# Row-group packing in the folds and the small attention, the score's two readers in the other order, and chunk 6's last sums ahead of the last finish

## The chip, the cores and the metric

The kernel runs on one core of one Trainium2 chip (trn2). The metric is device time in microseconds (us) of one launch; lower is better. The kernel before the change has a median of 2024.21 us over three runs (2023.55 to 2026.4).

TensorE (PE in the profile) multiplies matrices into PSUM, VectorE (DVE) and ScalarE (ACT) read PSUM and compute, GpSimd (POOL) computes on SBUF, and SyncE (SP) issues transfers. Each engine works through its own queue in order.

## The reference

Everything is float32. `x` is 16 samples of 64 latents of width 128 (1024 tokens), `ctx_1024` is 16 samples of 1601 context rows of width 128. Two layers run after each other:

```python
x = x + xattn0(ctx_1024, layernorm(x))            # 16 heads of 64; keys = context and latents
x = x + scan0(layernorm(x))                       # selective scan, width 256, 16 states
x = x + moe(layernorm(x))                         # small attention (4 heads of 32, one shared K and V), then top-2 of 8 experts
x = x + xattn1(ctx_1024, layernorm(x), mask)      # as xattn0, with a mask on context rows
x = x + scan1(layernorm(x))                       # convolution, 4 heads of 64, state 64
x = x + ffn(layernorm(x))                         # weights and activations quantized to fp4 in blocks of 16
```

For the change two pieces matter. The cross attention's projections are folded first: per head, `Wq_h Wk_h^T` and `Wv_h Wo_h` are 128x128 matrices, each a product over 64 rows. The small attention in `moe` is

```python
Q = (nx @ Wq.T) in 4 heads of 32;  K = nx @ Wkc.T;  V = nx @ Wvc.T     # K, V: 32 wide, the same for all heads
out = softmax(Q K^T / sqrt(32)) V per head;  X = X + concat(out) @ Wo.T
```

over samples of 64 tokens.

## The kernel before

The kernel is one program without loops on the chip; Python writes out every instruction. The tokens are 8 chunks of 128 (two samples each). The cross attention has 64 groups: 2 layers x 16 samples x 2 halves of the heads. A group has 13 context tiles of 128 rows (`NT`), and 8 heads x 64 latents make 512 columns (`NQ`).

`run` counts ticks `n`. Each tick (`step`) writes one tile's score (`scores`, L638 on: a matmul of 512 columns into one of three PSUM buffers of the pool `pss`) and, 21 ticks later (`LAG`), four matmuls of 129 columns that average the context with the weights of a tile (`average`). In between, a group's running maximum is turned (`maximum`, L674), spread (`mb`, L692), subtracted (L700) and exponentiated (L701).

A score in PSUM has two readers. ScalarE copies it to SBUF as `st` (L656 with the mask of layer 1, L658 in layer 0), and VectorE takes it into the running maximum `R` (L663 with the mask, L665 without). Both read the same PSUM bank, and the tile framework puts two readers from different engines on one bank in the order in which they are written: the copy first, then the maximum. The buffer is free for the score three ticks later when both are through.

Other work is written by generators between ticks. `prep` holds what the attention needs (latents, queries, context tiles, folds), `between` holds the stages after it: `scan0` and `moe` for four groups of two chunks in layer 0, then `scan1` and `ffn` in layer 1 for chunks 0-1, 2-3, 4-5, 6 and 7. A generator's `yield` gives a due time in ticks or a cost against a budget. Instructions written under `behind` may not be placed ahead of the last tick's. These stages use PSUM tiles of the pool `pst` (`tp`, three buffers that go round).

`fold` (L329 on) makes the folded matrices, four heads at a time: 2 layers x 2 products x 4 groups of heads. `raw_pair` loads 64 rows of four heads to 64 partitions; four matmuls over 64 rows (L341) fill one PSUM tile, and one instruction of 512 columns brings it out (L344 on ScalarE for the first two, else L346 on VectorE).

The small attention of `moe` works on two chunks (256 tokens, 4 samples). Queries are made per head on 32 partitions (`mq`, L929: 4 matmuls of 256 columns); keys (`mk`, L936) and values (`mv`, L940) follow. Scores `ms` (L951) are 8 matmuls over 32 rows, weights are turned (`mt`, L970), averaged (`ma`, L979: 8 matmuls over 64 rows with 32 output rows), copied (L982) and projected (`mo`, L988: 8 matmuls over 32 rows, four added up for each chunk).

At the end, `finish` (L726 on) brings the last group's average out, turns it and adds the output projection `o` (L785) to X. After the last tick `run` takes the remaining stages in turn: `tails` holds the chain of chunk 7's `scan1` and `ffn`, and the chain of what is left of chunk 6. Chunk 6's `ffn` ends with four matmuls `fo` (L1399), a sum into X (L1400) and the store (L1401). Chunk 7's `scan1` begins with a layer norm: `bn_stats` (L144), POOL's power (L135) and the scaling (L162). `fill` (L130) are matmuls without a use[...].

Of the kernel before, what the change touches and what calls it, by code (L numbers as in the profile page):

```python
# [32 lines left out]
F32 = mybir.dt.float32  # L33
# [3 lines left out]
AF = mybir.ActivationFunctionType  # L37
# [5 lines left out]
P = 128  # L43
# [30 lines left out]
CG = 2  # L74
# [5 lines left out]
class Kernel:  # L80
# [79 lines left out]
    def scaled(self, eng, dst, src, mv, r, n):  # L160
        for c in range(n):
            eng.tensor_scalar(dst[:, c, :], src[:, c, :], mv[:, c, 0:1], r[:, c:c + 1], ALU.subtract, ALU.mult)  # L162
# [154 lines left out]
    def raw_pair(self, lay, l, r, g, queue):  # L317


        if lay == 0:  # L320
            t = self.at.tile([P, 2, NQ], F32, tag="st2", name=f"raw{l}{g}", bufs=11)
            pair = [t[:DH, i, :].rearrange("p (h d) -> p h d", h=4) for i in range(2)]
        else:
            pair = [self.at.tile([DH, 4, D], F32, tag="raw", name=f"raw{n}{g}", bufs=3) for n in (l, r)]
        for t, n in zip(pair, (l, r)):
            queue.dma_start(out=t, in_=self.a[f"L{lay}{n}"].rearrange("(h j) d -> j h d", j=DH)[:, g * 4:g * 4 + 4, :])
        return pair

    def fold(self, lay, dst, l, r, scale):  # L329

        nc = self.nc
        for g in range(H // 4):
            if (lay, l) == (0, "WqT"):
                raw = self.raw0[g]
            else:
                raw = self.raw_pair(lay, l, r, g, nc.sync)
            if lay == 0 and l == "WvT":
                yield HOP3
            t = self.tp(f"{l}{lay}{g}")
            for k in range(4):  # L340
                nc.tensor.matmul(t[:, k * D:(k + 1) * D], raw[0][:, k, :], raw[1][:, k, :], start=True, stop=True)  # L341
# [296 lines left out]
    def scores(self, g, i):  # L638
# [15 lines left out]
        if masked:  # L654
            mc = self.mcol[:, i, b:b + 1]
            ev = nc.scalar.activation(st, s, AF.Identity, bias=mc)  # L656
        else:
            ev = nc.scalar.copy(st, s)  # L658
        self.place["ACT"].append(ev.ins)
        if i:  # L660
            last = grp["st"][0][:, 0, :] if i == 1 else R
            if masked:
                mx = nc.vector.scalar_tensor_tensor(R, s, mc, last, ALU.add, ALU.max)  # L663
            else:
                mx = nc.vector.tensor_tensor(R, s, last, ALU.max)  # L665
            self.place["DVE"].append(mx.ins)

# [236 lines left out]
    def moe(self, gr):  # L904
        nc, tc, a = self.nc, self.tc, self.a
        X = self.X[:, gr * CG:(gr + 1) * CG, :]
        with tc.tile_pool(name="mo1", bufs=1) as one, tc.tile_pool(name="mo2", bufs=2) as work:
# [3 lines left out]
            fWoT = ld("fWoT", [32, 4, D], a["fWoT"].rearrange("(h k) n -> k h n", k=32))  # L911
# [12 lines left out]
            q, kT, v = t1([32, BG, 4, L], "q"), t1([32, TG], "kT"), t1([L, BG, 32], "v")  # L924
            for hh in range(2):
                t = self.tp(f"mq{hh}")
                for k in range(2):
                    h = hh * 2 + k
                    nc.tensor.matmul(t[:32, k * TG:(k + 1) * TG], fWqT[:, h * 32:(h + 1) * 32], xT, start=True, stop=True)  # L929
                nc.scalar.copy(  # L930
                    q[:, :, hh * 2:hh * 2 + 2, :],
                    t[:32, :].rearrange("p (h b l) -> p b h l", h=2, l=L),
                )
                yield 0.7
            t = self.tp("mk")
            nc.tensor.matmul(t[:32, :TG], fWkvT[:, :32], xT, start=True, stop=True)  # L936
            nc.scalar.copy(kT, t[:32, :TG])
            t = self.tp("mv")
            for b in range(BG):
                nc.tensor.matmul(t[:L, b * 32:(b + 1) * 32], xT[:, b * L:(b + 1) * L], fWkvT[:, 32:], start=True, stop=True)  # L940
            nc.scalar.copy(v.rearrange("p b n -> p (b n)"), t[:L, :BG * 32])
# [6 lines left out]
            t = self.tp("ms")  # L948
            for i in range(n):
                b, hp = i // 2, i % 2  # L950
                nc.tensor.matmul(t[:, i * L:(i + 1) * L], q[:, b, 2 * hp:2 * hp + 2, :].rearrange("p h l -> p (h l)"), kT[:, b * L:(b + 1) * L], start=True, stop=True)  # L951
            t3 = t.rearrange("p (n l) -> p n l", l=L)
            m = self.sm([P, n], "mm")
            nc.vector.tensor_reduce(m, t3, AX.X, ALU.max)
            nc.vector.tensor_tensor(sc, t3, self.bc(m, shape), ALU.subtract)
            nc.scalar.activation(sc, sc, AF.Exp, scale=32.0 ** -0.5)
            yield 1.4
# [7 lines left out]
            oT = t1([32, 4, TG], "oT")  # L965
            pts = []
            for g in range(n // 4):
                t = self.tp(f"mt{g}")
                for i in range(4):
                    nc.tensor.transpose(t[:L, i * P:(i + 1) * P], sc[:, g * 4 + i, :], self.ident)  # L970
                pt = work.tile([L, 512], F32, tag="pt", name=f"mpt{g}")
                nc.vector.tensor_copy(pt, t[:L, :])
                pts.append(pt)
                yield 0.7
            yield HOP
            for g, pt in enumerate(pts):
                o = self.tp(f"ma{g}")
                for i in range(4):
                    nc.tensor.matmul(o[:32, i * P:(i + 1) * P], v[:, g * 2 + i // 2, :], pt[:, i * P:(i + 1) * P], start=True, stop=True)  # L979
                for j in range(2):  # L980
                    b = g * 2 + j
                    nc.scalar.copy(oT[:, :, b * L:(b + 1) * L], o[:32, j * 256:(j + 1) * 256].rearrange("p (h l) -> p h l", h=4))  # L982
                yield 0.1
            yield HOP
            o = self.tp("mo")
            for k in range(CG):
                for h in range(4):
                    nc.tensor.matmul(o[:, k * D:(k + 1) * D], oT[:, h, k * P:(k + 1) * P], fWoT[:, h, :], start=(h == 0), stop=(h == 3))  # L988
# [369 lines left out]
    def ffn(self, c0, CG):  # L1358
# [3 lines left out]
        with tc.tile_pool(name="ff1", bufs=1) as one, tc.tile_pool(name="ff2", bufs=CG) as work:  # L1362
# [37 lines left out]
            nc.vector.tensor_tensor(X, X, o[:, :CG * D].rearrange("p (c d) -> p c d", c=CG), ALU.add)  # L1400
# [4 lines left out]
    def run(self, out):  # L1405
# [39 lines left out]
        live = []  # L1445
        n, go, budget, finished = 0, 0, 0.0, 0
        while n < (ng + 1) * NT + LAG + 8 or between:
# [21 lines left out]
            if n >= 0:  # L1469
# [68 lines left out]
    def step(self, n, ng):  # L1538
# [96 lines left out]
```

## Time and profile before

| what | us |
|---|---|
| median of three runs | 2024.21 |
| the profiled execution's own time | 2023.47 |
| its span, first to last instruction | 2021.7 |
| PE busy | 1974.8 (98%) |
| DVE busy | 1563.8 (77%) |
| ACT busy | 1382.3 (68%) |
| POOL busy | 520.5 (26%) |
| granted TensorE clock, mean over the span | 0.996 |
| average `av`, PE | 868.1 |
| score `s`, PE | 853.0 |
| folds L341, PE (four rows of the groups) | 19.3 |
| `mq`, `mk`, `mv`, `ms`, `ma`, `mo`, PE | 7.8, 2.4, 2.6, 8.0, 7.7, 8.2 |

One float32 matmul stands in the profile as two instructions (LDWEIGHTS and MATMUL twice). "Mean ns" of a MATMUL holds the way through the array; what matmuls in a row cost is the distance between their starts. In a group, the numbers stand for busy time, mean ns of one, and the engine's idle time before them with what ended it. In the timeline, the columns are start, length and engine; a line merges instructions of one kind that follow each other.

### The profile page before, as it was taken

How to read it: one execution, taken by the hardware profiler on the slowest of the kernel's cores; microseconds unless marked ns; L12 is line 12 of the kernel's file. 1: busy time of each engine (PE TensorE's matmuls, PEld its weight loads, DVE VectorE, ACT ScalarE, POOL GpSimd, SP SyncE). 2: the span in 40 equal slices, each digit the busy share in tenths (PEclk: the TensorE clock that was granted, in tenths of full speed). 3: DMA queues.
4: the chain of work that ended last, by engine and by line, in shares of the span. 5: the costliest groups of instructions: out<-in, count | busy, mean ns of one | idle time of the engine just before them, and what ended most of it. 6: DMA issues, size and time to landing. Idle time of an engine off the chain costs nothing. (4 is left out here: it accounts for less than half of the span.)

```text
span 2021.7 us, 32901 instructions
## 1 busy us (share of the span) xinstructions
PE 1974.8 (98%) x12123; PEld 1499.8 (74%) x12123; DVE 1563.8 (77%) x2954; ACT 1382.3 (68%) x2628; POOL 520.5 (26%) x579
## 2 busy tenths in 40 slices
PE   9999999999999989999999999999999999999998
PEld 6777777676777767778777787777778777787787
DVE  6977777886778887676988777898686979778884
ACT  5788878887768887566767657776565656666561
POOL 5111123542123442121543203542111121002000
PEclk9999999999999999999999999999999999999999
DMA  6111112321122321221221102221110110101000
GB/s 175 63 59 46 46 42 84 84 73 50 43 66 84 83 70 36 65 76 45 67 80 51 36 24 72 71 62 51 44 53 18 57 36 22 55 18 36 23 1 22
DMA packets 141805, 110.54 MB, mean 55 GB/s; under 512 B 11458, under 2 KB 127950, under 8 KB 141646
## 3 DMA queue, kind: packets, MB, share of 16 engines
q1 hardware_dynamic: 141102, 108.19, 18.5%
q8 instruction: 96, 1.57, 0.3%
q14 instruction: 63, 0.52, 0.1%
q10 hardware_dynamic: 544, 0.26, 0.0%
HBM read 79.97 MB, written 27.41 MB: 53 GB/s over the span
## 5 line engine op out<-in xcount | busy, mean ns | idle before, releaser
L713 PEld LDWEIGHTS av<-kv,st 128*128 128x128 f32 x6656 | 851.6, 192 | 317.3 <-issue 288.7
L713 PE MATMUL av<-kv,st 128*128 128x129 f32 x6656 | 868.1, 276 | 6.5 <-DVE aq L722 3.9
L651 PE MATMUL s<-qT,kvT 128*128 128x512 f32 x1664 | 853.0, 602 | 17.2 <-DVE R L665 14.2
L700 DVE TENSOR_TENSOR st<-st,mb 128x1024 f32<-128x1024 f32 (+1 forms) x448 | 501.7, 1132 | 1.3 <-PE mb L692 1.1
L701 ACT ACTIVATE st<-st 128x1024 f32<-128x1024 f32 (+1 forms) x448 | 444.9, 997 | 72.1 <-DVE st L700 68.8
L656 ACT ACTIVATE st<-s,mcol 128x512 f32<-128x512 f32 x416 | 283.5, 685 | 221.2 <-PE s L651 178.6
L658 ACT COPY st<-s 128x512 f32<-128x512 f32 x416 | 240.3, 581 | 130.4 <-PE s L651 103.1
L651 PEld LDWEIGHTS s<-qT,kvT 128*128 128x128 f32 x1664 | 259.6, 192 | 84.8 <-DVE R L665 36.1
L663 DVE SCALAR_TENSOR_TENSOR R<-s,mcol,R 128x512 f32<-128x512 f32 x352 | 262.0, 744 | 69.8 <-ACT st L656 68.4
L665 DVE TENSOR_TENSOR R<-s,R 128x512 f32<-128x512 f32 x352 | 240.9, 685 | 90.4 <-ACT st L658 89.3
L762 POOL TENSOR_TENSOR aq<-aq,rd 128x512 f32<-128x512 f32 x63 | 77.6, 1232 | 409.9 <-DVE rd L761 402.6
L565 POOL TENSOR_TENSOR kv<-kv,vec 128x384 f32<-128x384 f32 (+1 forms) x128 | 137.6, 1094 | 151.0 <-PE kt L625 71.7
L866 POOL TENSOR_TENSOR db<-sc_u,bb 128x512 f32<-128x512 f32 x64 | 84.7, 1326 | 134.4 <-DVE h L877 60.8
L883 POOL TENSOR_TENSOR sc_y<-sc_y,h 128x512 f32<-128x512 f32 x60 | 79.9, 1332 | 104.2 <-DVE h L882 80.0
L877 DVE TENSOR_TENSOR_SCAN h<-da,db 128x512 f32<-128x512 f32 x64 | 85.3, 1333 | 0.0
L616 ACT ACTIVATE kv<-kv,coff,crstd 128x128 f32<-128x128 f32 x182 | 76.5, 489 | 5.1 <-POOL coff L613 5.1
L665 DVE TENSOR_TENSOR R<-s,st 128x512 f32<-128x512 f32 x32 | 22.1, 689 | 72.3 <-ACT st L658 72.3
L607 ACT ACTIVATE scr<-kv,cmean 128x128 f32<-128x128 f32 x182 | 72.8, 400 | 6.9 <-DVE cmean L603 3.7
L722 DVE SCALAR_TENSOR_TENSOR aq<-xeb,ee,av 128x129 f32<-128x129 f32 x252 | 72.8, 341 | 1.4 <-PE av L713 1.3
L135 POOL TENSOR_TENSOR crstd<-cvar,neghalf 128x13 f32<-128x13 f32 x14 | 35.0, 2502 | 134.6 <-DVE cvar L611 134.4
L450 PE MATMUL q<-xnT,wqk 128*128 128x128 f32 x512 | 68.8, 277 | 0.0
L450 PEld LDWEIGHTS q<-xnT,wqk 128*128 128x128 f32 x512 | 62.9, 192 | 6.3 <-issue 3.1
(410 smaller groups left out, 1973.5 us busy)
## 6 DMA issues: line engine op xcount, KB each, us to landing
bb<-bcd SPq DMA_DIRECT2D x64, 256.0 KB, 4.4
xh<-kv SPq DMA_DIRECT2D x16, 832.0 KB, 4.8
kv<-xh SPq DMA_DIRECT2D x16, 832.0 KB, 5.5
kvT<-xhT SPq DMA_DIRECT2D x16, 800.0 KB, 4.5
xhT<-kvT SPq DMA_DIRECT2D x15, 800.0 KB, 3.4
kv<-in_ctx_dram SPq DMA_DIRECT2D x15, 768.0 KB, 5.5
ew<-in_e1T_dram SPq DMA_DIRECT2D x36, 64.0 KB, 1.9
ew<-in_e3T_dram SPq DMA_DIRECT2D x36, 64.0 KB, 1.9
```

Source lines behind the costliest of these rows:

```text
L450: nc.tensor.matmul(t[:, k * P:(k + 1) * P], self.wqk[:, g * 4 + k, :], xnT, start=True, stop=True)
L565: nc.gpsimd.tensor_tensor(kv[:, lo:hi, :D], kv[:, lo:hi, :D], self.row(self.vec[:, w1, :], [P, hi - lo, D]), ALU.mult)
L651: mm = nc.tensor.matmul(s, self.kv_of[lay, b][1][:, i * P:(i + 1) * P], q, start=True, stop=True)
L656: ev = nc.scalar.activation(st, s, AF.Identity, bias=mc)
L658: ev = nc.scalar.copy(st, s)
L663: mx = nc.vector.scalar_tensor_tensor(R, s, mc, last, ALU.add, ALU.max)
L665: mx = nc.vector.tensor_tensor(R, s, last, ALU.max)
L700: nc.vector.tensor_tensor(st, st, self.row(mb, [P, n, NQ]), ALU.subtract)
L701: nc.scalar.activation(st, st, AF.Exp)
L713: nc.tensor.matmul(o, st, self.kv_of[lay, b][0][:, i, :], start=(i == 0 and k % 2 == 0), stop=(i == NT - 1 and k % 2 == 1))
L866: nc.gpsimd.tensor_tensor(db, u, self.row(bb[:, 0, s % 2, :], both), ALU.mult)
L877: nc.vector.tensor_tensor_scan(flat(h), flat(da), flat(db), 0.0, ALU.mult, ALU.add)
```

## The change

It has four parts.

1. In `scores` the maximum is written ahead of the copy.
2. `raw_pair` and `fold` put head 2m on partitions 0-63 and head 2m+1 on partitions 64-127. Matmuls alternate between the two halves, and each half has a PSUM tile of its own and an instruction of 256 columns that brings it out.
3. The small attention keeps four heads on four groups of 32 partitions: one query matmul of 128 output rows; a key weight repeated four times (four more loads), so that every group of partitions holds K; scores as 16 matmuls per two chunks of 32 rows x 64 output rows, in two PSUM tiles; averages as 4 matmuls of 256 columns on two halves of the rows; one projection matmul for each chunk.
4. `ffn` of a single chunk that isn't the last one yields ahead of its last sum. Ahead of the last `finish`, `upto_sums` writes the rest of chunk 6 up to that point. After the last tick, chunk 7's chain is advanced three steps first, and chunk 6's last sum is ordered behind the latest scaling of a layer norm.

```diff
     def scaled(self, eng, dst, src, mv, r, n):
         for c in range(n):
-            eng.tensor_scalar(dst[:, c, :], src[:, c, :], mv[:, c, 0:1], r[:, c:c + 1], ALU.subtract, ALU.mult)
+            self.normed = eng.tensor_scalar(dst[:, c, :], src[:, c, :], mv[:, c, 0:1], r[:, c:c + 1], ALU.subtract, ALU.mult)
...
         if lay == 0:
             t = self.at.tile([P, 2, NQ], F32, tag="st2", name=f"raw{l}{g}", bufs=11)
-            pair = [t[:DH, i, :].rearrange("p (h d) -> p h d", h=4) for i in range(2)]
+            pair = [t[:, i, :2 * D].rearrange("p (m d) -> p m d", m=2) for i in range(2)]
         else:
-            pair = [self.at.tile([DH, 4, D], F32, tag="raw", name=f"raw{n}{g}", bufs=3) for n in (l, r)]
+            pair = [self.at.tile([P, 2, D], F32, tag="raw", name=f"raw{n}{g}", bufs=3) for n in (l, r)]
         for t, n in zip(pair, (l, r)):
-            queue.dma_start(out=t, in_=self.a[f"L{lay}{n}"].rearrange("(h j) d -> j h d", j=DH)[:, g * 4:g * 4 + 4, :])
+            queue.dma_start(out=t, in_=self.a[f"L{lay}{n}"].rearrange("(m p) d -> p m d", p=P)[:, 2 * g:2 * g + 2, :])
...
-            t = self.tp(f"{l}{lay}{g}")
-            for k in range(4):
-                nc.tensor.matmul(t[:, k * D:(k + 1) * D], raw[0][:, k, :], raw[1][:, k, :], start=True, stop=True)
-            to = dst[:, g * 4:g * 4 + 4, :].rearrange("p h d -> p (h d)")
-            if (lay, l) == (0, "WqT") and g < 2:
-                nc.scalar.activation(to, t, AF.Copy, scale=scale)
-            else:
-                nc.vector.tensor_scalar_mul(to, t, scale)
+            ts = [self.tp(f"{l}{lay}{g}{i}") for i in range(2)]
+            for m in range(2):
+                for i in range(2):
+                    half = slice(i * DH, (i + 1) * DH)
+                    nc.tensor.matmul(ts[i][:, m * D:(m + 1) * D], raw[0][half, m, :], raw[1][half, m, :], start=True, stop=True)
+            for i in range(2):
+                to = dst[:, g * 4:g * 4 + 4, :].rearrange("p (m i) d -> p i m d", i=2)[:, i]
+                t = ts[i][:, :2 * D].rearrange("p (m d) -> p m d", m=2)
+                if (lay, l) == (0, "WqT") and g < 2:
+                    nc.scalar.activation(to, t, AF.Copy, scale=scale)
+                else:
+                    nc.vector.tensor_scalar_mul(to, t, scale)
...
         masked = lay == 1
-        if masked:
-            mc = self.mcol[:, i, b:b + 1]
-            ev = nc.scalar.activation(st, s, AF.Identity, bias=mc)
-        else:
-            ev = nc.scalar.copy(st, s)
-        self.place["ACT"].append(ev.ins)
+        mc = self.mcol[:, i, b:b + 1] if masked else None
+
         if i:
...
             self.place["DVE"].append(mx.ins)
+        if masked:
+            ev = nc.scalar.activation(st, s, AF.Identity, bias=mc)
+        else:
+            ev = nc.scalar.copy(st, s)
+        self.place["ACT"].append(ev.ins)
...
-            fWoT = ld("fWoT", [32, 4, D], a["fWoT"].rearrange("(h k) n -> k h n", k=32))
+            fWoT = ld("fWoT", [P, D])
+            fWk4 = t1([P, 4, 32], "fWk4")
+            for i in range(4):
+                nc.sync.dma_start(out=fWk4[:, i, :], in_=a["fWkvT"][:, :32])
...
-            q, kT, v = t1([32, BG, 4, L], "q"), t1([32, TG], "kT"), t1([L, BG, 32], "v")
...
+            q, kT, v = t1([P, TG], "q"), t1([P, TG], "kT"), t1([P, CG, 32], "v")
+            t = self.tp("mq")
+            nc.tensor.matmul(t[:, :TG], fWqT, xT, start=True, stop=True)
+            nc.scalar.copy(q, t[:, :TG])
...
+            nc.tensor.matmul(t[:, :TG], fWk4.rearrange("p r n -> p (r n)"), xT, start=True, stop=True)
...
             for b in range(BG):
+                nc.tensor.matmul(t[b % 2 * L:(b % 2 + 1) * L, b // 2 * 32:(b // 2 + 1) * 32], xT[:, b * L:(b + 1) * L], fWkvT[:, 32:], start=True, stop=True)
...
+            ts = [self.tp(f"ms{i}") for i in range(2)]
+            for b in range(BG):
+                for h in range(4):
+                    rows, tok = slice(h * 32, (h + 1) * 32), slice(b * L, (b + 1) * L)
+                    nc.tensor.matmul(ts[h // 2][h % 2 * L:(h % 2 + 1) * L, tok], q[rows, tok], kT[rows, tok], start=True, stop=True)
+            for i in range(2):
+                t3, mi, half = ts[i][:, :TG].rearrange("p (n l) -> p n l", l=L), m[:, i * BG:(i + 1) * BG], [P, BG, L]
+                nc.vector.tensor_reduce(mi, t3, AX.X, ALU.max)
+                nc.vector.tensor_tensor(sc[:, i * BG:(i + 1) * BG, :], t3, self.bc(mi, half), ALU.subtract)
...
+            oT = t1([P, TG], "oT")
+            pt = work.tile([P, 512], F32, tag="pt", name="mpt", bufs=1)
...
+            for c in range(CG):
+                for i in range(2):
+                    rows = slice(i * L, (i + 1) * L)
+                    nc.tensor.matmul(ts[i][:32, c * 256:(c + 1) * 256], v[rows, c, :], pt[rows, c * 256:(c + 1) * 256], start=True, stop=True)
+            to = oT.rearrange("p (c i l) -> p i c l", i=2, l=L)
+            for i in range(2):
+                o = ts[i][:32, :].rearrange("p (c h l) -> p h c l", c=CG, l=L)
+                for h in range(4):
+                    nc.scalar.copy(to[h * 32:(h + 1) * 32, i], o[:, h])
...
-                for h in range(4):
-                    nc.tensor.matmul(o[:, k * D:(k + 1) * D], oT[:, h, k * P:(k + 1) * P], fWoT[:, h, :], start=(h == 0), stop=(h == 3))
+                nc.tensor.matmul(o[:, k * D:(k + 1) * D], oT[:, k * P:(k + 1) * P], fWoT, start=True, stop=True)
...
+            alone = CG == 1 and not last
+            if alone:
+                self.summed = True
+                yield 0.0
+            x = nc.vector.tensor_tensor(X, X, o[:, :CG * D].rearrange("p (c d) -> p c d", c=CG), ALU.add)
+            if alone:
+                self.later(x, self.normed)
...
+        def upto_sums():
+            while not self.summed:
+                with self.behind(1):
+                    if next(between[0][2], None) is None:
+                        between.pop(0)
...
+                    self.trace(tails[0], 3)
...
-                (self.finish if ga == ng - 1 else self.gather)(ga)
+                if ga == ng - 1:
+                    self.upto_sums()
+                    self.finish(ga)
+                else:
+                    self.gather(ga)
```

More of the change, by code (lines that the diff above doesn't have):

```diff
@@ L922, in moe @@
             yield HOP
-            q, kT, v = t1([32, BG, 4, L], "q"), t1([32, TG], "kT"), t1([L, BG, 32], "v")
[L925 to L934, printed above, removed]
+            q, kT, v = t1([P, TG], "q"), t1([P, TG], "kT"), t1([P, CG, 32], "v")
+            t = self.tp("mq")
+            nc.tensor.matmul(t[:, :TG], fWqT, xT, start=True, stop=True)
+            nc.scalar.copy(q, t[:, :TG])
+            yield 0.4
             t = self.tp("mk")
-            nc.tensor.matmul(t[:32, :TG], fWkvT[:, :32], xT, start=True, stop=True)
-            nc.scalar.copy(kT, t[:32, :TG])
+            nc.tensor.matmul(t[:, :TG], fWk4.rearrange("p r n -> p (r n)"), xT, start=True, stop=True)
+            nc.scalar.copy(kT, t[:, :TG])
             t = self.tp("mv")
             for b in range(BG):
-                nc.tensor.matmul(t[:L, b * 32:(b + 1) * 32], xT[:, b * L:(b + 1) * L], fWkvT[:, 32:], start=True, stop=True)
-            nc.scalar.copy(v.rearrange("p b n -> p (b n)"), t[:L, :BG * 32])
+                nc.tensor.matmul(t[b % 2 * L:(b % 2 + 1) * L, b // 2 * 32:(b // 2 + 1) * 32], xT[:, b * L:(b + 1) * L], fWkvT[:, 32:], start=True, stop=True)
+            nc.scalar.copy(v.rearrange("p b n -> p (b n)"), t[:, :CG * 32])
             yield 0.3
@@ L947, in moe @@
             sc = t1(shape, "sc")
[L948 to L952, printed above, removed]
-            m = self.sm([P, n], "mm")
-            nc.vector.tensor_reduce(m, t3, AX.X, ALU.max)
-            nc.vector.tensor_tensor(sc, t3, self.bc(m, shape), ALU.subtract)
+            m = self.sm([P, n], "mm")
+            ts = [self.tp(f"ms{i}") for i in range(2)]
[7 more added lines that the diff above has]
+                nc.vector.tensor_tensor(sc[:, i * BG:(i + 1) * BG, :], t3, self.bc(mi, half), ALU.subtract)
             nc.scalar.activation(sc, sc, AF.Exp, scale=32.0 ** -0.5)
-            yield 1.4
+            yield 1.6
             yield HOP1
@@ L964, in moe @@
             yield HOP
[L965 to L973, printed above, removed]
+            oT = t1([P, TG], "oT")
+            pt = work.tile([P, 512], F32, tag="pt", name="mpt", bufs=1)
+            for j in range(2):
+                t = self.tp(f"mt{j}")
+                for c in range(CG):
+                    for i in range(2):
+                        nc.tensor.transpose(t[:L, (c * 2 + i) * P:(c * 2 + i + 1) * P], sc[:, i * BG + 2 * c + j, :], self.ident)
+                nc.vector.tensor_copy(pt[j * L:(j + 1) * L], t[:L])
                 yield 0.7
             yield HOP
[L976 to L982, printed above, removed]
+            ts = [self.tp(f"ma{i}") for i in range(2)]
+            for c in range(CG):
+                for i in range(2):
+                    rows = slice(i * L, (i + 1) * L)
+                    nc.tensor.matmul(ts[i][:32, c * 256:(c + 1) * 256], v[rows, c, :], pt[rows, c * 256:(c + 1) * 256], start=True, stop=True)
+            to = oT.rearrange("p (c i l) -> p i c l", i=2, l=L)
+            for i in range(2):
+                o = ts[i][:32, :].rearrange("p (c h l) -> p h c l", c=CG, l=L)
+                for h in range(4):
+                    nc.scalar.copy(to[h * 32:(h + 1) * 32, i], o[:, h])
                 yield 0.1
@@ L1399, in ffn @@
                     nc.tensor.matmul(o[:, k * D:(k + 1) * D], hT[k][:, i * P:(i + 1) * P], self.wdT[:, i, :], start=(i == 0), stop=(i == 3))
-            nc.vector.tensor_tensor(X, X, o[:, :CG * D].rearrange("p (c d) -> p c d", c=CG), ALU.add)
+            alone = CG == 1 and not last
[5 more added lines that the diff above has]
+                self.later(x, self.normed)
             nc.sync.dma_start(out=self.out.rearrange("(c p) d -> p c d", p=P)[:, c0:c0 + CG, :], in_=X)
@@ L1445, in run @@
         live = []
+        def upto_sums():
[3 more added lines that the diff above has]
+                        between.pop(0)
+        self.summed, self.upto_sums = False, upto_sums
         n, go, budget, finished = 0, 0, 0.0, 0
```

## The prediction

> **What bounds the kernel now.** I read the page's busy shares and costliest groups first, then the timeline of TensorE alone, then the waits at scores, then the last 40 us.
>
> ```profile
> PE 1974.8 (98%) x12123; PEld 1499.8 (74%) x12123; DVE 1563.8 (77%) x2954; ACT 1382.3 (68%) x2628; POOL 520.5 (26%) x579
> ...
> L713 PE MATMUL av<-kv,st 128*128 128x129 f32 x6656 | 868.1, 276 | 6.5 <-DVE aq L722 3.9
> L651 PE MATMUL s<-qT,kvT 128*128 128x512 f32 x1664 | 853.0, 602 | 17.2 <-DVE R L665 14.2
> ...
> L663 DVE SCALAR_TENSOR_TENSOR R<-s,mcol,R 128x512 f32<-128x512 f32 x352 | 262.0, 744 | 69.8 <-ACT st L656 68.4
> L665 DVE TENSOR_TENSOR R<-s,R 128x512 f32<-128x512 f32 x352 | 240.9, 685 | 90.4 <-ACT st L658 89.3
> ```
>
> TensorE is the bound: what is taken off its queue comes off the time, as long as VectorE and ScalarE follow, and both have a quarter to a third of the span free. VectorE's idle time ahead of the maximum is time spent behind ScalarE's copy of the same score. The page's busy time hides stalls inside a matmul's way through the array. From single start times, gaps of over 0.15 us beyond what a matmul's columns take come to 61 us in 92 places; 23.6 us of them, in 29 places, stand ahead of a score.
>
> What small matmuls cost is seen between starts (pieces of TensorE's timeline: the fold, a product that is already split over two halves of the rows, then `mq`, `ms`, `ma`, `mo`):
>
> ```profile
> 823.16 1.16 PE L341 MATMUL WqT<-rawWkT,rawWqT 64*128 64x128 f32 x8
> 824.25 1.16 PE L713 MATMUL av<-kv,st 128*128 128x129 f32 x8
> ...
> 1540.47 0.72 PE L1250 MATMUL gr<-sd_cT,sd_bT 64*128 64x128 f32 x8
> 1541.12 1.12 PE L651 MATMUL s<-qT,kvT 128*128 128x512 f32 x2
> ...
> 488.16 1.91 PE L929 MATMUL mq<-mo_xT,w_fWqT 128*32 128x256 f32 x8
> 489.91 0.59 PE L936 MATMUL mk<-mo_xT,w_fWkvT 128*32 128x256 f32 x2
> ...
> 495.98 1.99 PE L951 MATMUL ms<-mo_kT,mo_q 32*128 32x64 f32 x16
> 497.91 0.27 PE L629 MATMUL kt_r<-ident,kv 64*128 64x64 f32 x1
> ...
> 510.12 1.93 PE L979 MATMUL ma<-mpt,mo_v 64*32 64x128 f32 x16
> 511.99 0.70 PE L651 MATMUL s<-qT,kvT 128*128 128x512 f32 x1
> ...
> 515.69 2.05 PE L988 MATMUL mo<-w_fWoT,mo_oT 32*128 32x128 f32 x16
> 517.66 0.70 PE L651 MATMUL s<-qT,kvT 128*128 128x512 f32 x1
> ```
>
> Eight fold instructions take 824.25 - 823.16 = 1.09 us; eight of the same size on alternating halves (`gr`) take 0.65. Single `gr` starts come in pairs 13 ns apart, pairs 0.11 us apart, plus 0.2 us at the change of shape: both halves run at once.
>
> [...] `mo` with 32 rows moves on every 0.11 us, as `av` with 128 does, so a K of 32 saves nothing by itself. [...] a maximum starts 0.03 us after the copy when it waits for it.
>
> **The change part by part**, against the span of 2021.7 us. That execution took 2023.47 in all (1.8 around the span); the median is 0.7 above it.
>
> Small attention, each of four token groups:
> - `mq`: eight instructions in 1.75 us become two of the same 0.22 us: -1.31.
> - `mk` keeps its count: 0. The repeated weight is four more transfers of SP, ahead of the layer norm that feeds `mk`; SP has room (its queue waits tens of us at a time). 0; if they were late, `mk` would wait about 2 us.
> - `mv`: eight in 0.58, now in pairs of column halves. `se` (L406), paired so, starts 6 ns apart. -0.15.
> - `ms`: 16 instructions in 1.93 become 32 with 64 columns of weights on four row groups. `mv`, with 64 columns of weights, moves on every 0.058 us; a row group gets eight, 0.46, plus 0.2 for the mode: 0.65. -1.28 (all in a row: 32 x 0.058 + 0.2 = 2.06, +0.13).
> - `ma`: 16 in 1.87 become eight of 256 columns on two halves: 4 x 0.22 + 0.2 = 1.08, -0.79 (in a row 1.95, +0.08).
> - `mo`: 16 in 1.97 become four of 0.11: -1.53.
>
> Sum 5.06, four times: **-20.2**. Without overlap it is 4 x (1.31 + 1.53 - 0.13 - 0.08) = -10.5. Readers beside it: ScalarE copies 256 instead of 1024 columns for `mq` (-0.77) and eight small pieces instead of four of 357 ns for `oT` (+0.7); VectorE splits two 0.69 us instructions into four (+0.2). They lie beside attention matmuls.
>
> Folds: 16 x (1.09 - 0.65) = -7.0. Four of them (1.75) lie in the first 17 us, where TensorE also waits for transfers and copies: half counts. **-6.1**. Bringing out two halves costs VectorE some 0.15 us each more, beside matmuls.
>
> Chunk 6's end:
>
> ```profile
> 1986.08 0.54 POOL L135 TENSOR_TENSOR rstd<-var,neghalf 128x1 f32<-128x1 f32 x1 [18.11 <-DVE var L155]
> 1986.51 1.06 PE L1399 MATMUL fo<-wdT,fh 88*128 88x128 f32 x8
> 1987.60 0.29 DVE L1400 TENSOR_TENSOR X<-X,fo 128x128 f32<-128x128 f32 x1 [1.60 <-PE fo L1399]
> 1987.81 0.34 DVE L162 TENSOR_SCALAR sd_xi<-X,mv,rstd 128x128 f32<-128x128 f32 x1
> ```
>
> The scale is ready at 1986.62, but VectorE stands in L1400, which waits for `fo` behind the fill: 1.1 us of the last chain. Moved, `fo` (0.9 us) falls into TensorE's wait of 1.09 us ahead of L745, its input being ready at 1980.64; L1400 (0.29) comes ahead of the last sum of `o`, while VectorE waits 1.96 us for that. The store and the loads behind it on SP start earlier. On POOL the memset of chunk 7's padding now stands ahead of the power and waits for L1400, which is over some 3 us before the power's input: 0. **-1.1**. If `fh` were late, `fo` would hold the finish by up to 0.9.
>
> Maximum first: VectorE no longer waits for ScalarE (161.5 + 121.5 us in the waits); ScalarE's copy waits for the maximum, and exponentials and context work queue behind it. Where ScalarE was late, the buffer comes free about 0.7 us earlier:
>
> ```profile
> 755.40 0.56 ACT L658 COPY st<-s 128x512 f32<-128x512 f32 x1
> 756.00 0.69 DVE L665 TENSOR_TENSOR R<-s,R 128x512 f32<-128x512 f32 x1 [2.79 <-ACT st L658]
> 756.74 1.12 PE L651 MATMUL s<-qT,kvT 128*128 128x512 f32 x2 [2.70 <-DVE R L665]
> ```
>
> Here TensorE would start at 756.0. But of 42 releases that the next score met within 0.15 us, only 5 are like this; in 37 the maximum began as VectorE came free, so the copy (0.58 to 0.69) would now follow it. These stand in some 24 clusters; at 0.75 each that is +18. Against it, in 32 of the 42 VectorE's run of work began with a maximum that had waited for a copy (0.1 to 2.8 us, mostly near 1), and it now begins sooner. I take **+2**, ends -10 and +18.
>
> New waits: TensorE arrives 5 us sooner for each small attention's inputs (it already waits 4.5 us at `mot`), and two PSUM tiles of three are held at once. **+2** (0 to 5). The clock stood at half from 830.7 to 837.5 us right after `mo` with 32 rows and a fold with 64, 3.4 us lost; half a chance that it goes: **-1.7**.
>
> Sum: -20.2 - 6.1 - 1.1 + 2 + 2 - 1.7 = -25.1. Span 1996.6, profiled execution 1998.4, median **1999**.
>
> **The rivals.**
> - Score releases grow later, without the compensation: +18 for +2, 2015. For: 37 of 42. Against: VectorE's 283 us of waits are gone. 14%.
> - The order helps more than thought, -10 for +2: 1987. For: 23.6 us of stalls. 11%.
> - Row groups don't overlap: -10.5 for -20.2 and no fold gain, 2015. `gr` speaks against it. 5%.
> - Slower: static replacement holds everywhere. With each copy put after its maximum, 75 scores find their buffer late, by 37.3 us in sum. +37.3 for +2: 2034. It decides once the added waits pass 27 us. For: TensorE, faster, leaves the chain less slack. Against: waits in a cluster overlap. 6%.
> - My forecast has 64%, its own range 1991 to 2008.
>
> **How the numbers follow.** The range 1986 to 2015 takes in half of each neighbour. Measurement tells about 0.2% (4 us) from no change: faster 0.92 (all but the slower rival and the outer edge of the first), same 0.04, slower 0.04.
>
> **What would show it.** `fold` eight instructions in about 0.65 us; `ms` in 0.65, `ma` in 1.1, `mo` in 0.45; TensorE's busy time down by about 25 us; waits of the maximum for the copy gone and the copy's waits for `R` in their place; scores waiting for `st`, in sum near the old 17 to 24 us (over 40: the slower rival); L162 of chunk 7 right after its POOL power. I am wrong if `ms` stays near 2 us, or if stalls ahead of scores double.

## The result, and the profile after

The changed kernel took 1986.94 us (median of six runs, 1984.66 to 1991.68) beside 2023.88 for the kernel before (six runs, 2013.49 to 2026.4): ratio 0.9835, 95% interval 0.9818 to 0.9852. It is faster, as forecast: the interval lies below 1. I had said 1999, and the time lies only 0.9 us above the lower end of my range (1986). Beside later experiments, 49 more runs of the kernel before gave a median of 2019.90 and five more of the changed kernel 1985.34, just below that end. So it took some luck for the range to hold, and the gain is 33 to 35 us rather than the 37 between the first medians. The forecast was 25. The missing 8 to 10 us are what the experiments had to find.

The profiled execution took 1984.66 us, its span is 1983.0 (before 2021.7), the mean granted clock 0.999 (before 0.996). The busy shares and costliest groups of the changed kernel's page:

```profile
PE 1938.7 (98%) x12083; PEld 1476.6 (74%) x12083; DVE 1557.6 (79%) x2976; ACT 1380.2 (70%) x2642; POOL 516.1 (26%) x579
...
L719 PE MATMUL av<-kv,st 128*128 128x129 f32 x6656 | 866.3, 275 | 3.2 <-DVE aq L728 2.5
L656 PE MATMUL s<-qT,kvT 128*128 128x512 f32 x1664 | 850.6, 599 | 16.0 <-ACT st L671 8.7
...
L669 ACT ACTIVATE st<-s,mcol 128x512 f32<-128x512 f32 x416 | 283.8, 683 | 217.3 <-DVE R L664 173.5
L671 ACT COPY st<-s 128x512 f32<-128x512 f32 x416 | 240.5, 580 | 132.5 <-DVE R L666 101.1
...
L664 DVE SCALAR_TENSOR_TENSOR R<-s,mcol,R 128x512 f32<-128x512 f32 x352 | 261.8, 744 | 42.3 <-PE s L656 40.8
L666 DVE TENSOR_TENSOR R<-s,R 128x512 f32<-128x512 f32 x352 | 240.5, 683 | 44.4 <-PE s L656 43.7
```

TensorE is busy 36 us less (about 25 was forecast). The maximum no longer waits for the copy; it waits for the score itself, and the copy waits for the maximum. Scores are now released by the copy, but their idle time, 16.0 us, is about the old 17.2. Ahead of `av` it has halved, from 6.5 to 3.2. That line turned out to matter.

Pieces of TensorE's timeline in the changed kernel, start and length in us: one fold, then `ms`, `ma` and `mo`, each with the instruction that follows:

```profile
812.98 0.71 PE L344 MATMUL WqT<-rawWkT,rawWqT 64*128 64x128 f32 x8
813.63 0.49 PE L719 MATMUL av<-kv,st 128*128 128x129 f32 x2
...
489.51 0.69 PE L957 MATMUL ms<-mo_kT,mo_q 32*64 32x64 f32 x32
490.13 1.12 PE L656 MATMUL s<-qT,kvT 128*128 128x512 f32 x2
...
502.55 1.05 PE L986 MATMUL ma<-mpt,mo_v 64*32 64x256 f32 x8
503.54 1.98 PE L656 MATMUL s<-qT,kvT 128*128 128x512 f32 x4
...
507.14 0.61 PE L996 MATMUL mo<-w_fWoT,mo_oT 128*128 128x128 f32 x4
507.59 1.02 PE L656 MATMUL s<-qT,kvT 128*128 128x512 f32 x2
```

Start to next start: the fold 0.65 us (1.09 before), `ms` 0.62 (1.93), `ma` 0.98 (1.87), `mo` 0.45 (1.97). Row groups overlap here: within `ms`, starts on the four groups follow each other by 5 to 7 ns, where the 32-row `mo` of the kernel before moved on every 0.11 us.

Chunk 6's end in the changed kernel's timeline:

```profile
1942.82 1.10 PE L1407 MATMUL fo<-wdT,fh 88*128 88x128 f32 x8
1943.02 0.16 DVE L743 TENSOR_TENSOR den<-av,ee 128x4 f32<-128x4 f32 x1 [1.63 <-PE av L719]
...
1945.00 0.28 DVE L1412 TENSOR_TENSOR X<-X,fo 128x128 f32<-128x128 f32 x1
...
1948.15 0.54 POOL L135 TENSOR_TENSOR rstd<-var,neghalf 128x1 f32<-128x1 f32 x1 [4.02 <-DVE var L155]
1948.73 0.34 DVE L162 TENSOR_SCALAR sd_xi<-X,mv,rstd 128x128 f32<-128x128 f32 x1 [0.66 <-POOL rstd L135]
```

The scaling (L162) starts 0.04 us after POOL's power has ended, as forecast; before it stood 1.19 us behind it, in VectorE's queue behind L1400, which waited 1.60 us for `fo`.

Two tables of my own counting serve below. The first sums, for one trace of each kernel, TensorE's stalls: time of over 0.15 us between two starts beyond what the first one's columns take at the clock of that moment. (The prediction's 61 us in all and 23.6 at scores were counted at full speed everywhere; they are 57.0 and 21.7 in this count.) `mot` are the transposes of the layer norm ahead of the small attention, `WqT` and `WvT` the folds, `kt` the transposes of context tiles, `q` the queries of the cross attention.

| us of stalls ahead of | scores | `av` | `mot` | `WqT`, `WvT` | `kt`, `q`, `mv`, `mk` | all |
|---|---|---|---|---|---|---|
| kernel before | 21.7 | 9.1 | 4.5 | 2.1 | 0.7 | 57.0 |
| order alone (e1) | 24.7 | 4.0 | 1.9 | 1.5 | 4.2 | 52.8 |
| changed kernel | 20.8 | 4.9 | 1.9 | 6.2 | 4.0 | 54.1 |
| the same again (e5) | 22.0 | 4.6 | 1.9 | 4.4 | 3.7 | 52.1 |
| all but the order (e6) | 18.8 | 8.8 | 4.3 | 4.1 | 1.7 | 57.9 |

The second is about the clock. Single runs of one kernel differ by up to 12 us, and their mean granted clock says which way: for the kernel before 2023.4 us at 0.995 (11 runs), 2021.2 at 0.996 (16), 2017.8 at 0.997 (5), 2016.6 at 0.998 (8), 2014.8 at 0.999 (8). That is 2.1 us for each 0.001. Where I write "at equal clock", runs with the same mean clock are compared.

### The profile page after: what moved, and what is told of

Its sections match the earlier page's. It is cut to its first block, busy times and chain, and to the rows that moved or that the text cites. A ratio compares the mean times of both kernels' runs of the same rounds, so it can differ in the third digit from the quotient of the medians.

```text
span 1983.0 us, 32835 instructions
## 1 busy us (share of the span) xinstructions
PE 1938.7 (98%) x12083; PEld 1476.6 (74%) x12083; DVE 1557.6 (79%) x2976; ACT 1380.2 (70%) x2642; POOL 516.1 (26%) x579
## 3 DMA queue, kind: packets, MB, share of 16 engines
q1 hardware_dynamic: 143406, 108.46, 18.8%
## 5 line engine op out<-in xcount | busy, mean ns | idle before, releaser
L570 POOL TENSOR_TENSOR kv<-kv,vec 128x384 f32<-128x384 f32 (+1 forms) x128 | 132.2, 1054 | 169.3 <-DMA xh<-kv 63.9
L768 POOL TENSOR_TENSOR aq<-aq,rd 128x512 f32<-128x512 f32 x63 | 71.4, 1134 | 354.6 <-DVE rd L767 349.3
L889 POOL TENSOR_TENSOR sc_y<-sc_y,h 128x512 f32<-128x512 f32 x60 | 86.0, 1434 | 98.1 <-DVE h L888 81.5
```

Source lines behind the costliest of these rows:

```text
L570: nc.gpsimd.tensor_tensor(kv[:, lo:hi, :D], kv[:, lo:hi, :D], self.row(self.vec[:, w1, :], [P, hi - lo, D]), ALU.mult)
L889: nc.gpsimd.tensor_tensor(y, y, h, ALU.add)
```

## The experiments

My theory before them: the 37 us are 27 of packing, some 7 of half-speed stretches of the clock that went, and 1 of the last chain; the order of the readers gives nothing. The rival: the order brings what my sum lacked.

**Each part alone.** The kernel before with one part of the change each; the edits are the parts of the diff above:

```
 e1, scores
-        ev = nc.scalar.copy(st, s)
         mx = nc.vector.tensor_tensor(R, s, last, ALU.max)
+        ev = nc.scalar.copy(st, s)
 e2, moe (with all that belongs to it)
-        ... t[:32, k * TG:(k + 1) * TG], fWqT[:, h * 32:(h + 1) * 32], xT
+        ... t[:, :TG], fWqT, xT
 e3, raw_pair and fold
-        ... t[:, k * D:(k + 1) * D], raw[0][:, k, :], raw[1][:, k, :]
+        ... ts[i][:, m * D:(m + 1) * D], raw[0][half, m, :], raw[1][half, m, :]
 e4, the last tick and tails
-        (self.finish if ga == ng - 1 else self.gather)(ga)
+        if ga == ng - 1:
+            self.upto_sums()
+            self.finish(ga)
```

> The kernel before with one part of the change alone: the maximum of a score is issued and ordered ahead of its copy. My theory: the change gained 37 us by packing (27), by half-speed stretches of TensorE's clock that went (about 7) and by the last chain (1), and the order of the two readers is worth nothing by itself: within 5 us of the kernel before, stalls ahead of scores between 17 and 28 us in sum (23.6 before). Rival, the order brings the ten us that my sum did not have: 10 to 14 us faster than before, stalls ahead of scores under 15 us. Second rival, copies behind maxima hold the buffers longer and the packing merely pays for that: 8 to 18 us slower.

> The kernel before with the packing of small attention alone. Theory: TensorE is the bound and takes 8.62 us between starts for these six products of one token group before, 3.28 in the changed kernel: 21 us faster than before for four groups, or up to 25 if the half-speed stretch of the clock that followed the product with 32 rows goes as well. Rival, the freed TensorE runs into VectorE and ScalarE, and the readers' new order is needed to use it: 8 to 14 us faster, with more and longer stalls ahead of scores than 23.6 us.

> The kernel before with the folds on two halves of the rows alone. Theory: eight instructions 0.44 us shorter for each of twelve folds in the stream of work, and little for the four at the start: 5 us faster than before. Rival, the folds' loads or their two pieces of output take it back: 0 to 2 us faster. Rival from the clock, a fold with 64 rows sets off the half-speed stretch: 8 to 9 us faster, with no such stretch in its trace after 830 us.

> The kernel before with chunk 6's last product and sum ahead of the last finish alone. Theory: 1.1 us faster than before, too little for the medians to tell; in the trace the normalising of chunk 7 (L162 or its line here) starts right after its power on POOL, and from the last denominator of attention to the last sum into X it takes 36.7 us for 37.9. Rival, the wait comes back later in the chain: that stretch stays at 37.9 us.

| | median us (runs) | ratio to before, 95% interval | us by the ratio | at equal clock |
|---|---|---|---|---|
| before | 2019.90 (49) | | | |
| e1, order | 2013.58 (22) | 0.9974, 0.9965 to 0.9984 | -5.3 | -3 to -6, mean -4.0 |
| e2, small attention | 1999.00 (5) | 0.9898, 0.9882 to 0.9914 | -20.6 | -19.4 and -20.0 |
| e3, folds | 2015.44 (12) | 0.9978, 0.9966 to 0.9990 | -4.4 | -1.9 to -4.4, mean -2.5 |
| e4, end | 2019.58 (22) | 0.9994, 0.9983 to 1.0005 | -1.2 | not to be told |

Small attention and folds are near the theory. Of the folds' 5 us part is given back: in e3's trace a stall of 2.0 us ahead of `tm` at 39.8 us is new. The end isn't seen in the medians, but its stretch of the trace (last denominator to last sum into X) is 36.65 us for 37.86, as expected.

The order is where both stories fell. It isn't worth nothing, since the interval excludes that, and it isn't worth ten. And it doesn't act where I looked: stalls ahead of scores did not fall (they grew by 3.0 us, 2.1 of them in one place at 42.5 us), those ahead of `av` and `mot` fell by 7.7. Ahead of `av` this holds in all traces: 8.6 to 9.1 us in the six with the copy first in both layers, 4.0 to 4.9 in the six with the maximum first. One place shows how. Ahead of the first token group's `mot`, the kernel before has in its timeline:

```profile
474.04 2.04 ACT L616 ACTIVATE kv<-kv,coff,crstd 128x128 f32<-128x128 f32 x5 [0.36 <-POOL coff L613]
...
475.09 0.42 DVE L901 TENSOR_TENSOR X<-X,po 128x256 f32<-128x256 f32 x1
...
475.98 0.57 ACT L658 COPY st<-s 128x512 f32<-128x512 f32 x1
...
476.58 0.69 DVE L665 TENSOR_TENSOR R<-s,R 128x512 f32<-128x512 f32 x1 [1.07 <-ACT st L658]
...
477.19 0.48 DVE L144 BATCH_NORM_STATS2 bs<-X 128x6 f32<-128x128 f32 x2
...
481.59 0.60 PE L177 MATMUL mot<-ident,mo_nx 128*128 128x128 f32 x2 [2.49 <-DVE mo_nx L162]
```

and the changed kernel:

```profile
472.57 0.42 DVE L907 TENSOR_TENSOR X<-X,po 128x256 f32<-128x256 f32 x1
...
472.90 0.69 DVE L666 TENSOR_TENSOR R<-s,R 128x512 f32<-128x512 f32 x1
...
473.50 0.48 DVE L144 BATCH_NORM_STATS2 bs<-X 128x6 f32<-128x128 f32 x2
...
477.92 0.30 PE L177 MATMUL mot<-ident,mo_nx 128*128 128x128 f32 x1 [1.04 <-DVE mo_nx L162]
```

In the kernel before the score's copy is queued behind five scalings of context tiles on ScalarE (2.04 us), the maximum waits 1.07 us for the copy, and the layer norm's statistics stand behind the maximum on VectorE. TensorE then waits 2.49 us for that layer norm. With the maximum first, VectorE isn't tied to ScalarE's queue: from the sum into X to `mot` it takes 5.35 us instead of 6.50.

Ahead of `av` it is less simple. TensorE's list of groups has, in the kernel before and in e1, what ended its idle time there:

```profile
L713 PE MATMUL av<-kv,st 128*128 128x129 f32 x6656 | 868.1, 276 | 6.5 <-DVE aq L722 3.9 <-ACT kv L616 1.8 <-ACT st L701 0.8
L714 PE MATMUL av<-kv,st 128*128 128x129 f32 x6656 | 867.4, 275 | 2.4 <-DVE aq L723 1.6 <-ACT st L702 0.4
```

`aq` is VectorE's sum that brings a group's averages out of PSUM; its share fell by 2.3 us. ScalarE's share, scalings of context tiles (`kv`) and exponentials (`st`), fell by 2.2. Why that part came earlier was not followed up.

**The parts together, and the order undone.** e5 is the changed kernel again. e6 to e8 put the copy back in front, in both layers or in one:

```
 e6
+        ev = nc.scalar.copy(st, s)
         mx = nc.vector.tensor_tensor(R, s, last, ALU.max)
-        ev = nc.scalar.copy(st, s)
 e7, copy() being the same lines as a function
+        if masked: copy()
         mx = ...
+        if not masked: copy()
 e8
+        if not masked: copy()
         mx = ...
+        if masked: copy()
```

> The changed kernel, nothing edited, beside many runs of the kernel before on the same chip. Theory: the four parts alone gave 5.3, 20.6, 4.4 and 1.2 us by their ratios, 31.5 in sum, and the parts add up: ratio 0.983 to 0.985, 31 to 34 us; of these 29 us where runs with the same mean clock are compared, the rest because the mean clock of its runs is higher. Rival, the parts help each other: 37 us or more, as between the first medians.

> The changed kernel with the copy of a score ahead of its maximum again, all else kept. Theory, the order is worth what it was worth alone, through VectorE's other work: 4 to 5 us slower than the changed kernel at equal clock; stalls of over 0.15 us ahead of av (4.9 us in sum in the changed kernel) and of mot (1.9) go back to about 9 and 4.5, stalls ahead of scores stay within 18 to 23. Rival, with TensorE faster the buffers of the scores are the tighter place and the order matters more: 8 to 12 us slower, stalls ahead of scores over 28. Second rival, no effect once TensorE is packed: within 1 us.

> The changed kernel with the maximum ahead of the copy in layer 0's scores alone; in layer 1 (masked) the copy is first again. Theory, each layer has its share: half of the order's gain is lost, 2 us slower than the changed kernel, and half of the stalls ahead of av and mot come back. Rival, the gain is layer 0's alone and in layer 1 the copy had better stay first: 0 to 3 us faster than the changed kernel.

> The changed kernel with the maximum ahead of the copy in layer 1's scores alone; in layer 0 the copy is first again. Theory, each layer has its share: 2 us slower than the changed kernel, and what this kernel and the one with layer 0 alone lose adds up to what the kernel without the new order loses. Rival, the gain is layer 1's alone: 0 to 3 us faster than the changed kernel.

| | median us (runs) | ratio to before, 95% interval | against e5 |
|---|---|---|---|
| before | 2020.46 (9) | | |
| e5, changed kernel | 1985.34 (5) | 0.9828, 0.9809 to 0.9847 | |
| e6, copy first | 1992.70 (4) | 0.9871, 0.9851 to 0.9891 | +7.4 |
| e7, maximum first in layer 0 | 1990.22 (4) | 0.9859, 0.9838 to 0.9879 | +4.9 |
| e8, maximum first in layer 1 | 1988.52 (4) | 0.9846, 0.9826 to 0.9866 | +3.2 |

The whole is 34.8 us, a little more than the parts' 31.5, by less than the parts' intervals leave open. Of that the order is worth 7.4 beside the packing, 5 to 7 at equal clock, more than my theory's 4 to 5 and less than the rival's 8 to 12. The stalls ahead of `av` and `mot` go back to 8.8 and 4.3, those ahead of scores fall to 18.8: the theory's place, not the rival's.

Neither mixture of the orders (e7, e8) is faster than the change. Their losses, 4.9 and 3.2, add up to about the 7.4, but their intervals overlap with e5's; the traces tell more. Layer 0's scores end at 983 us in the kernel before. TensorE's timeline ahead of `mot` of the first and the last token group, in e7 (maximum first in layer 0) and then in e8 (in layer 1):

```profile
477.66 0.30 PE L177 MATMUL mot<-ident,mo_nx 128*128 128x128 f32 x1 [1.03 <-DVE mo_nx L162]
...
1365.31 0.64 PE L177 MATMUL mot<-ident,mo_nx 128*128 128x128 f32 x2 [0.64 <-ACT st L713]
...
482.10 0.59 PE L177 MATMUL mot<-ident,mo_nx 128*128 128x128 f32 x2 [2.49 <-DVE mo_nx L162]
...
1366.72 0.38 PE L177 MATMUL mot<-ident,mo_nx 128*128 128x128 f32 x2
```

Each wait is the short one where the maximum is first in the scores that run at the time, and the old one where the copy is. In sum, 4.1 us of stalls ahead of `av` and `mot` come back in e7 and 2.7 in e8, against the mean of the changed kernel's two traces: both layers have a share.

VectorE's longest waits in e6 are the old ones:

```profile
DVE R L670 <- ACT st L663: 148.3, 117, 6.6
DVE R L668 <- ACT st L661: 114.7, 106, 3.8
```

(total us, times, longest), while the changed kernel has in their place:

```profile
DVE R L666 <- PE s L656: 98.2, 69, 6.3
DVE R L664 <- PE s L656: 71.5, 76, 3.6
```

VectorE's waits at these two lines fell from 263 to 185 us, and 170 of what remains is waiting for TensorE, the bound.

**The clock.** In the trace of the kernel before, TensorE stood at half speed from 482.5, 759.0, 830.7 and 1718.1 us, for 3.4, 3.4, 6.8 and 3.4 us; counted as above, starts in these stretches came 8.0 us later than their columns need. The changed kernel's first trace has none ahead of 1980.2 us, when TensorE has nothing left to do, its second two (3.0 us). All stretches in all traces begin and end on a grid of 3.41 us that starts with the first full-speed stretch; the four starts above lie 276.5, 71.7 and 887.4 us apart, 81, 21 and 260 steps. For each window of the grid I summed its matmuls' time at full speed, weighted by the share of the 128 rows that each uses. Three kernels test what this suggests:

```
 e9   after:  t = self.tp(name)
 +            rows = {"mot1": 32, "mot2": P}.get(name, 0)
 +            for _ in range(60 if rows else 0):
 +                nc.tensor.matmul(t[:, :P], self.ident[:rows, :], self.ident[:rows, :], ...)
 e10  after:  self.scaled(nc.vector, nx, X, mv, rr, CG)
 +            for _ in range(gr + 1):
 +                nc.gpsimd.tensor_scalar_mul(nx, nx, 1.0)
 e11  before: t = self.tp(name)
 +            if name == "mot0":
 +                for _ in range(22):
 +                    nc.tensor.matmul(t[:, :P], self.ident, self.ident, ...)
```

> The changed kernel with 60 matmuls more of 128 columns that nobody reads, ahead of the second token group's transposes (mot) with 32 rows of the array, ahead of the third's with all 128; each lot keeps TensorE busy for about 6.4 us. It tests what sets off a half-speed stretch of TensorE's clock. Theory from the ten traces so far: the clock is set for windows of 3.41 us on a fixed grid, and a window runs at half speed when the work of the one before, each matmul's time weighted by its share of the 128 rows, filled less than about 0.38 of it (17 of 17 windows below 0.36 were followed by half speed, none of 5733 others that lay above 0.44 was spared wrongly). Then a half-speed stretch of one or two windows follows the 32-row lot (weight 0.25) although TensorE was never idle, and none follows the 128-row lot; about 13 us for the matmuls and 2 to 5 for the clock more than the changed kernel. Rival, only idle time counts: no half-speed stretch after either lot, 13 us. Second rival, the stretches come at random: no relation.

> The changed kernel with the layer norm's output ahead of mot passed through GpSimd once, twice, three and four times (multiplied by 1) for token groups 0 to 3, so that TensorE waits longer there each time, by about 1.5 us a pass. Theory of the windows: a wait of over 4.3 us always leaves some window under 0.38 and is followed by half speed, one of under 2.1 us never is, between them it depends on where the grid lies; so half speed after groups 2 and 3, and the cost of each wait is its length and up to 1.7 us more for each half-speed window: about 15 us of waits and 4 to 8 for the clock. Rival, the clock doesn't follow waits: 15 us and no half-speed stretch at these places.

> The kernel before with 22 matmuls of 128 columns and 128 rows that nobody reads (2.35 us) put into TensorE's wait of 2.66 us ahead of the first token group's transposes, which half speed followed in that kernel's trace (482.5 us). Theory of the windows: the wait stays but is filled, the window at 479 us is no longer under 0.38, and no half-speed stretch follows there; 1.3 to 1.7 us faster than before, less than the medians can tell. Rival, the stretch belongs to that place in the program: it stays.

e9 took 2021.64 us (12 runs; ratio to before 1.0011, 1.0000 to 1.0022). Each matmul of 128 columns in fp32 is two instructions, so each lot has 120 and lasts twice what I had written. TensorE's timeline in e9:

```profile
775.68 21.48 PE L178 MATMUL mot<-ident 32*128 32x128 f32 x120
797.09 0.69 PE L180 MATMUL mot<-ident,mo_nx 128*128 128x128 f32 x2
...
1104.55 13.56 PE L178 MATMUL mot<-ident 128*128 128x128 f32 x120
1117.95 0.38 PE L180 MATMUL mot<-ident,mo_nx 128*128 128x128 f32 x2
```

and four windows around them, with TensorE's busy time and count first and its granted clock in the third column from the end:

```profile
core 0: us, PE busy (x) PEld busy (x) DVE busy (x) ACT busy (x) POOL busy (x), PEclk, DMA share, GB/s
770.50:775.00 4.50, 4.50 (x25) 3.07 (x25) 4.05 (x9) 3.29 (x5) 1.31 (x4) 1.00 0.21 50
777.20:780.60 3.40, 3.40 (x33) 3.40 (x32) 3.40 (x6) 3.40 (x10) 0.00 (x0) 1.00 0.49 139
780.70:801.10 20.40, 20.40 (x85) 18.11 (x84) 1.39 (x4) 4.81 (x9) 0.72 (x1) 0.50 0.01 1
...
1105.00:1117.90 12.90, 12.90 (x118) 12.90 (x117) 7.32 (x8) 7.44 (x8) 0.00 (x0) 1.00 0.15 41
```

In these windows TensorE was busy without a gap in both lots (20.40 of 20.40 us and 12.90 of 12.90). After one window of 32-row work the granted clock was 0.50 and stayed there for six windows, until 801.1; under the same number of 128-row instructions it was 1.00 throughout. Idle time alone therefore doesn't account for the stretches, and the rival falls. The lots took 21.4 and 13.4 us, so half speed cost the first lot 8.0 us; the two together are the 35 us by which e9 is slower than the changed kernel.

e11 took 2022.01 us (20 runs; ratio 1.0007, 0.9998 to 1.0016). No half-speed stretch follows at 482 us: TensorE was busy for all of the 3.40 us from 479.1 (0.91 in the kernel before), and the clock granted from 482.6 was 1.00 (0.50 before). The place alone doesn't make it. The filler is twice as long as I had reckoned, though (44 instructions, `mot` at 483.80 us instead of 481.59), which takes the gain back; so the theory's -1.3 to -1.7 us was not tested.

e10 took 1993.96 us (4 runs; ratio 0.9872, 0.9850 to 0.9894), 7 to 9 more than the changed kernel. The waits ahead of `mot` grew to 1.80, 2.40, 2.63 and 3.56 us only, all under the 4.3 that I had called certain (like the 2.1, an estimate of mine from the 3.41 us and the 0.38: 0.62 of a window, and about twice that for a wait that the grid cuts in half), and no half speed followed them: the four windows had weighted work of 0.39 to 0.44. The expectation for groups 2 and 3 failed because the waits were shorter than planned. At 49.7 us, where a stall of 3.0 us left a window with 0.07, half speed did follow. Stalls ahead of `mot` rose from 1.9 to 10.4 us in sum, which is the whole of the loss.

Over 14 traces, from 20 to 1940 us: of the windows with weighted work under 0.375, 27 of 27 were followed by a half-speed window; from 0.375 to 0.44 it was 5 of 32; above, none of some 7,800. Unweighted, windows of up to 0.95 are among those followed; weighted by rows and columns, windows of up to 0.39 are, and one of 0.30 isn't. Of the three counts, in these traces, only the one by rows has every window under 0.375 followed and none above 0.44.

**Where the folds lost.** The value folds of layer 0 as they were, all else changed:

```
 e12  fold:  +            if lay == 0 and l == "WvT":
             +                t = self.tp(f"{l}{lay}{g}")
             +                for k in range(4): nc.tensor.matmul(...)   # 64 rows, one tile
```

> The changed kernel with the value folds of layer 0 alone (four of sixteen) as they were before, eight instructions on 64 rows into one PSUM tile; the other twelve stay packed. Theory: these four gain almost nothing from packing, because two of them are cut into two lots of four instructions at 0.61 to 0.64 us a lot (3.6 us for the four, 4.3 before), and they pay for the second PSUM tile with waits (stalls ahead of WvT 3.2 us in sum in the changed kernel's first trace, 1.7 in its second, 1.1 before; ahead of kt 1.3 to 1.6, 0.2 before): 1 to 2 us faster than the changed kernel at equal clock, about 1983 to 1986, stalls ahead of WvT and kt together about 1.3 us. Rival, the packing pays here as elsewhere and the stalls only move to other instructions: 0 to 1 us slower, about 1986 to 1988.

1989.26 us (5 runs; ratio 0.9843, 0.9819 to 0.9866): not faster, though the interval overlaps with e5's. The stalls ahead of `WvT` and `kt` went from 4.8 us (2.9 in e5) to 1.3 as the theory said, but another stands ahead of a score in its trace. e1, the other kernel with these folds unpacked and the maximum first, has the same (second line):

```profile
38.60 2.08 PE L668 MATMUL s<-qT,kvT 128*128 128x512 f32 x2 [2.35 <-ACT st L683]
...
42.51 1.22 PE L651 MATMUL s<-qT,kvT 128*128 128x512 f32 x1 [2.35 <-ACT st L666]
```

Four half-speed windows follow in each, from 38.2 and 41.7 us on, with 64-row folds in them. At clocks of 0.998 and 0.999 its two runs, 1986.8 and 1986.6, are level with or 1 us behind the changed kernel's. The traces speak for the rival, that the stall moved; one microsecond is less than these medians can tell. There is no reason to unpack these folds.

## Why the prediction was right or wrong

- **Small attention, -20.2: right.** Alone -20.6 (-17.4 to -23.8 by the interval). From start to next start the six products of a group went from 8.62 to 3.28 us, four times -5.34: -21.4. Reading `gr`'s pairs of starts as proof of overlap was sound, and taking `mv`'s 0.058 us for `ms` too (0.65 said, 0.62 measured). The 0.2 us "for the mode" are the step at the change of shape in the trace of the kernel before (0.20 us ahead of and behind `gr` and behind `mo`, where 0.11 is usual). `mk`, said to stay, lost 0.09.
- **Folds, -6.1: too large.** A fold takes 0.65 us as said, but the sixteen together went from 18.2 us (0.9 of it one fold at half speed) to 13.0, because some wait in the middle or are cut into two lots of four (0.61 to 0.64 us each) in the stream of layer 0. Alone they gave -4.4 (-2.0 to -6.9).
- **Chunk 6's end, -1.1: right** in the traces (36.65 us for 37.86 in e4, the changed kernel and e5), under what medians show.
- **Maximum first, +2: wrong.** This is the step that failed. I priced the order at the scores only, by which buffer comes free when, and put VectorE's 283 us of waits into a sentence of "against". Ahead of scores the account was fair: neither +18 nor relief. But VectorE's queue also holds layer norms and the sums of `aq`, and TensorE waits for these. Freed of ScalarE's queue they came earlier, and part of ScalarE's own work did too: -4.2 us of stalls ahead of `av`, about half of that from `aq` by e1's list of waits, and -2.6 ahead of `mot`. Measured -5.3 alone and -7.4 beside the packing. The rival that the order helps by 10, with 1987 us and a chance of 11%, was nearer in sign and time than the forecast, though it too looked for the gain at the scores.
- **New waits, +2: low.** Stalls ahead of `WqT`, `WvT` and `mv` rose from 2.1 us to 6.0 and 7.8 in the two traces of the changed kernel. The trace shows one: at 49.1 us a fold waits 2.0 us for ScalarE's copy of `kt`, the third PSUM tile of three. The order has a share of the new waits too (`kt` and `q` in e1). Ahead of the folds they are not the packed folds' doing alone: e2, with unpacked folds, has 3.8 us there, e3, with packed ones, 0.7.
- **Clock, -1.7: low.** I counted one stretch at half a chance. All four left the first trace (8.0 us), and over the runs the mean clock rose from 0.9966 to 0.9982 (six runs) and 0.9990 (five): at 2.1 us for 0.001, -3.4 to -5.0. The rows of `mo`, which I suspected, fit e9, where 32-row work without a gap was followed by a clock of 0.50; long waits fit e11, where filling one took the clock behind it from 0.50 to 1.00.
- **Baseline.** I worked against a median of 2024.21 from three runs; 49 more gave 2019.90. Some 2 to 4 us of the first difference were the scatter of these few runs.
- **The other rivals.** Later releases (+18) and the slower case (+37.3) needed stalls ahead of scores to double; they stayed at 21 to 22 us. That row groups don't overlap is refuted by `ms`: 32 instructions in 0.62 us, where 16 took 1.93.

The four parts alone come to -31.5 us, measured together -33 to -35. At equal clock the whole is 29 to 30 us. So the sum of -25.1 lacked 5 to 9 us at the order and 2 to 3 at the clock (the larger figures for the order hold some of the clock), and held some 2 us too many at the folds. What the waits for a second PSUM tile cost apart from the order was not separated.

## What to carry to other kernels

Where two engines read one buffer in a fixed order, price the order by everything that stands in the second reader's queue, not only by when the buffer comes free: here a good part of the gain came through a layer norm just behind the maximum (2.6 us fewer stalls ahead of `mot`). What packing small products on row groups brings can be read off a product of the same kernel that is already split (`gr` took 0.65 us, and so does the packed fold). It may pay twice: in the kernel before, 6.8 us of half speed stood behind a 32-row `mo` and a 64-row fold (from 830.7 us), and the changed kernel's first trace has none there. When runs of one kernel scatter, look at each run's mean clock before comparing medians.

## What the runs showed of the hardware that was not expected

In these traces the half-speed stretches of TensorE's clock lay on a grid of 3.41 us, and they went with the work of the window before, in time weighted by rows: 27 of 27 windows below 0.375 were followed by a half-speed window, 5 of 32 from 0.375 to 0.44, none of some 7,800 above. A half-speed window cost 1.3 to 1.6 us of this kernel's work (8.0 us for five in the trace of the kernel before, 3.0 for two in e5, 8.0 for six in e9's 32-row lot).

The length of a stall, counted as in the first table, did not tell alone. In the kernel before, 2.14 us ahead of `at` at 1717.46 us, all in one window, were followed by half speed, and 1.97 us ahead of a score at 386.67, also in one window, were not. In the changed kernel 2.52 us ahead of `at` at 1681.54, which the grid cuts into 0.79 and 1.73, were not either. And e9's 32-row work was followed by half speed without any gap.
